# A transformer block on one core: scores in groups of three heads, V by halves, and the queue's products in column tiles

## The chip, the core and the metric

The kernel runs on one core of one Trainium2 chip. A core has a matrix engine (TensorE, PE in the profile), which reads its operands from SBUF and writes its products into PSUM; a vector engine (DVE); a scalar engine (ACT); GpSimd (POOL)[...]; and queues that start DMA transfers, here almost all from SyncE (SP). Each engine works through its own list of instructions, and semaphores order the lists among each other. [...] The metric is the time of one execution on the device in microseconds; a run's number is the median of several executions.

## The reference, cut to what matters

Attention and a feed-forward layer, each followed by a residual sum and a layer norm, over x of 4 x 2048 x 256 in fp32, 16 heads of 16 columns. The feed-forward layer rounds inputs, weights and the hidden values to FP4 in blocks of 16.

```python
q = split_heads(x @ Wq.T); k = split_heads(x @ Wk.T); v = split_heads(x @ Wv.T)
scores = jnp.einsum('bhld,bhmd->bhlm', q, k) * SCALE
attn = jax.nn.softmax(scores, axis=-1)
out = jnp.einsum('bhlm,bhmd->bhld', attn, v)
x = _layernorm(x + out.transpose(0, 2, 1, 3).reshape(B, L, D_MODEL) @ Wo.T)
gate = fp4_linear(x, w_gate); y = fp4_linear(x, w_up)
h = jax.nn.silu(gate) * y
x = _layernorm(x + fp4_linear(h, w_down))
```

## The kernel before, in words

**Steps and periods.** Attention goes by steps: one batch entry (4), one block of 512 queries (4 of them) and one group of four heads (4), 64 steps in all. Each step has 16 tiles of 128 keys (NKT), so there are 1024 periods, and each period treats one such tile, n, of one step.

**Scores twice.** The softmax is stabilised by the row maximum, and the scores are computed twice. First, `maxima` forms q rows by k columns (128 queries by 512 keys) for two heads at once into `pm`, a PSUM tile of two banks from the pool ps_m, which has two such tiles. One DVE reduce takes the maximum of both heads (line 397). `max_rows` later turns the maxima of a step round, and DMAs put them as two extra rows under q. Then `exponentials` forms the scores transposed (128 keys by 512 queries), one head to a bank of the pool ps_x (three banks), already with the maximum subtracted through the extra rows, and ACT takes the exponential (line 431) into SBUF tiles `e`, of which there are ten. The maxima run ahead of the exponentials by LEAD = 20 periods.

**Forms of the array.** The score products contract over 62 or 64 rows. Two heads stand in the upper and lower half of the array and run as a pair, which the profile shows as 62*128 and 64*128. `values` multiplies the exponentials by V: 128 keys contract, a head has 32 columns, and four heads stand next to each other in the array (128*32). They write four parts of one bank, `av`. The queue's products, such as pg, pu, pz, pq, pv and py, use the whole array (128*128), and so do nearly all transposes. An fp32 product is done in two passes, each with its own weight load, so the profile counts it twice; the score products (fp32r) take one.

**The queue.** All other work (projections, output projection and residual, feed-forward) stands in generators. `period(parts)` runs the steps that have come due, one part of each urgent generator (`max_rows`, `normalize`), and then parts of the queue until `parts` with a cost of at least LEAST have been run. `later(periods, step, rest)` puts a step off by so many calls of `period` and tells when its result may be used; `fp4` uses it between its halves. `psum` gives the queue its banks from the same three of ps_x that the exponentials use.

**The order of one period.** The loop at the end of the kernel writes this order, and each engine keeps it:

```python
for i in range(NP):
    if m < N: maxima(sm, im, i)
for i in range(NP):
    if 0 <= n < N: exponentials(s, kt, i)
    if i == 0 and n >= LAG: values(sv, kv)
...
period(1 if n >= 0 else 2)
```

On PE this is four products of maxima, two of exponentials, four of V (of the tile LAG = 2 periods back), two of exponentials, and then the queue's part.

The functions that the change touches, with the lines of the profile:

Of the kernel before, what the change touches and what calls it, by code (L numbers as in the profile page):

```python
# [31 lines left out]
F32 = mybir.dt.float32  # L32
# [18 lines left out]
FB = 16  # L51
LN_EPS = 1e-5
LEAD = 20
LAG = 2
LEAST = 300.0
PSUM = bass.MemoryType.PSUM
DRAM = bass.MemoryType.DRAM
# [16 lines left out]
def block_kernel(  # L74
# [55 lines left out]
            state["done"] = clock["now"]  # L130


    def matmul(*args, **kw):
        tc.keep_in_program_order(nc.tensor.matmul(*args, **kw))  # L134

    def transpose(*args):
        tc.keep_in_program_order(nc.tensor.transpose(*args))  # L137
# [7 lines left out]
    def fp4(pool, t, tag, gain=1.0, engine=None):  # L145

        p, nb, _ = t.shape
        amax = pool.tile([p, nb], F32, tag="amax" + tag, name="amax")
        nc.vector.tensor_reduce(amax, t, AX.X, ALU.max, apply_absolute_value=True)  # L149
        sc = pool.tile([p, nb], F32, tag="sc" + tag, name="sc")  # L150
        nc.vector.tensor_scalar(sc, amax, gain / 6.0, 1e-12, ALU.mult, ALU.max)
        rs = pool.tile([p, nb], F32, tag="rs" + tag, name="rs")
        nc.vector.reciprocal(rs, sc)
        engine = engine or nc.gpsimd
        engine.tensor_scalar(rs, rs, gain * TIES_DOWN, 1.0, ALU.mult, ALU.mult)
        xn = pool.tile([p, nb, FB], F32, tag="xn" + tag, name="xn", bufs=3 if tag else 2)
        engine.tensor_tensor(xn, t, rs.unsqueeze(2).to_broadcast([p, nb, FB]), ALU.mult)

        def rounded():
            m = pool.tile([p, nb, FB], F32, tag="m" + tag, name="m", bufs=1)  # L160
            nc.vector.tensor_single_scalar(m.bitcast(I32), xn.bitcast(I32), EXPONENT, ALU.bitwise_and)
            nc.vector.tensor_scalar(m, m, 1.0, ROUND, ALU.max, ALU.mult)  # L162
            engine.tensor_tensor(xn, xn, m, ALU.add)  # L163
            engine.tensor_tensor(xn, xn, m, ALU.subtract)  # L164
            engine.tensor_tensor(xn, xn, sc.unsqueeze(2).to_broadcast([p, nb, FB]), ALU.mult)  # L165

        return xn, later(1, rounded, 4 if tag == "" else 2)


    ident = const.tile([P, P], F32, tag="ident", name="ident")  # L170
# [178 lines left out]
            yield 900  # L349

    steps = [(b, qb, g) for b in range(B) for qb in range(NQB) for g in range(NG)]
    k_sb, q_sb, v_sb, mx_sb, av_ps, e_sb = {}, {}, {}, {}, {}, {}

    def load_q(s):
        b, qb, g = steps[s]
# [23 lines left out]
        v_sb[s] = p1.tile([P, NKT, NP * 3 * DH], F32, tag="v", name="v", bufs=2)  # L379
        nc.sync.dma_start(v_sb[s], vx[b % 2][g])  # L380

    def maxima(s, n, i):

        if n == 0 and i == 0:
            mx_sb[s] = p2.tile([P, QT, HG, NQB], F32, tag="mx", name="mx")
        kb, t = n // QT, n % QT
        pm = ps_m.tile([P, 2, QB], F32, tag="pm", name="pm")
        for j in range(2):
            rows = slice(R * j, R * j + RM)
            matmul(  # L390
                pm[:, j, :],
                q_sb[s, i][rows, t * P : (t + 1) * P],
                k_sb[s, i, kb][rows, :],
                start=True,
                stop=True,
            )
        nc.vector.tensor_reduce(mx_sb[s][:, t, 2 * i : 2 * i + 2, kb], pm, AX.X, ALU.max)  # L397

    def max_rows(s):

        nm = p2.tile([P, QT, HG], F32, tag="nm", name="nm")
        nc.vector.tensor_reduce(nm, mx_sb.pop(s), AX.X, ALU.max, negate=True)
        nh = p2.tile([P, QT, HG, 2], F32R, tag="nh", name="nh")
        nc.vector.tensor_copy(nh[:, :, :, 0], nm)
        nc.vector.tensor_tensor(nh[:, :, :, 1], nm, nh[:, :, :, 0].bitcast(F32), ALU.subtract)
        yield 0
        yield 0
        pn = psum("pn")
        for t in range(QT):
            transpose(  # L410
                pn[: 2 * HG, t * P : (t + 1) * P], nh[:, t].rearrange("p h c -> p (h c)").bitcast(F32), ident
            )
        nr = p2.tile([2 * HG, QB], F32R, tag="nr", name="nr", bufs=1)
        nc.scalar.copy(nr, pn[: 2 * HG, :])
        for i in range(NP):
            for j in range(2):
                h = 2 * i + j
                nc.sync.dma_start(
                    q_sb[s, i][R * j + RM : R * j + R, :].bitcast(F32), nr[2 * h : 2 * h + 2, :].bitcast(F32)
                )  # L420
        yield 400

    def exponentials(s, kt, i):
        kb, col = kt // QT, kt % QT * P
        pe = [psum("pe") for _ in range(2)]
        for j in range(2):
            rows = slice(R * j, R * j + R)
            matmul(pe[j], k_sb[s, i, kb][rows, col : col + P], q_sb[s, i][rows, :], start=True, stop=True)
        for j in range(2):
            e = p1.tile([P, QB], F32, tag="e", name="e", bufs=10)  # L430
            nc.scalar.activation(e, pe[j], AF.Exp, scale=SCALE)  # L431
            e_sb[s, kt, 2 * i + j] = e

    def values(s, kt):
        if kt == 0:
            av_ps[s] = ps_av.tile([P, QB], F32, tag="av", name="av")
        for j in range(HG):
            matmul(
                av_ps[s][S * j : S * j + S, :],
                v_sb[s][:, kt, (j // 2) * 3 * DH + v_at(j) : (j // 2) * 3 * DH + v_at(j) + S],  # L440
                e_sb.pop((s, kt, j)),
                start=(kt == 0),
                stop=(kt == NKT - 1),
            )

    oTs, oq_of = {}, {}
# [1 line left out]
    def normalize(s):  # L448

        av_sb = p2.tile([P, QB], F32, tag="av_sb", name="av_sb", bufs=1)  # L450
        nc.scalar.copy(av_sb, av_ps.pop(s))
        yield 0
        yield 0
        pa = psum("pa")
        for t in range(QT):
            transpose(pa[:, t * P : (t + 1) * P], av_sb[:, t * P : (t + 1) * P], ident)

        pairs = pa.rearrange("p (t i a d) -> p t i a d", t=QT, i=NP, d=DH)
        rd = p2.tile([P, QT, NP, 2], F32, tag="rd", name="rd")
        nc.vector.reciprocal(rd, pairs[:, :, :, 1:3, 0])  # L460
        if s % 2 == 0:
            oq_of[s // 2] = p2.tile([P, QT, P], F32, tag="oq", name="oq", bufs=1)
        oq = oq_of[s // 2].rearrange("p t (g i j d) -> p t g i j d", g=2, i=NP, d=DH)
        for i in range(NP):
            nc.vector.tensor_tensor(
                oq[:, :, s % 2, i],
                pairs[:, :, i, 0:4:3, :],
                rd[:, :, i, :].unsqueeze(3).to_broadcast([P, QT, 2, DH]),
                ALU.mult,
            )  # L470
        yield 500
        if s % 2 == 0:
            return
        yield 0
        pr = psum("pr")
        for t in range(QT):
            transpose(pr[:, t * P : (t + 1) * P], oq_of[s // 2][:, t, :], ident)
        oT = p1.tile([P, QB], F32, tag="oT", name="oT", bufs=3)
        nc.scalar.copy(oT, pr)
        oTs[s // 2] = oT  # L480
        yield 500
# [19 lines left out]
    def residual(b, qb, x1, xq):  # L501

        for t in range(QT):
# [10 lines left out]
            if t % 2:  # L514
                layer_norm(x1, t - 1, 2)
                tiles = x1[:, t - 1 : t + 1].rearrange("p t (b f) -> p (t b) f", f=FB)
                later(3, lambda tiles=tiles: xq.append(fp4(p2, tiles, "")))
            yield 900

    def gated(xqT, h, t, engine):  # L520
# [54 lines left out]
    def down(x1, hT, t):  # L575
        for n in range(KC):
            cols = slice(n * P, (n + 1) * P)
            pz = psum("pz")[:, :P]
            for c in range(NFC):
                w = min(P, FF - c * P)  # L580
                matmul(pz, hT[:w, t % 2, c, :], wdT[:w, c, cols], start=(c == 0), stop=(c == NFC - 1))
            nc.gpsimd.tensor_add(x1[:, t, cols], x1[:, t, cols], read(pz))  # L582
            yield 1300

    def feed_forward(b, qb, between):
# [23 lines left out]
        def gate(t):  # L609
# [2 lines left out]
            h = p2.tile([P, FF], F32, tag="h", name="h")  # L612
            yield from gated(xqT, h, t, engine)
            blocks = h.rearrange("p (b f) -> p b f", f=FB)
            later(1, lambda: hq.update({t: fp4(p2, blocks, "h", gain=0.5, engine=engine)}))

        def out_rows(t):
            layer_norm(x1, t, 2)
# [78 lines left out]
    others = [projection(0, tb, ("q0", "q1")) for tb in range(1, NQB)] + [projection(1, 0)]  # L697
    queue.append(weave(prepare(), chain_of(others), 2))

    for n in range(-LEAD, N + LAG):  # L700
        m = n + LEAD
        (sm, im), (s, kt), (sv, kv) = divmod(m, NKT), divmod(n, NKT), divmod(n - LAG, NKT)
        if m in (8, 10, 12, 14):
            if m == 8:
                load_q(1)
            load_k(1, m // 2 - 4)
        if n == 0:
            load_v(0)
        if kt == 3 and 0 <= n and s + 1 < len(steps):
            load_v(s + 1)  # L710
        if n > 0 and kt % QT == 0:
            ahead, kb = divmod(n - QT + 2 * NKT, NKT)
# [6 lines left out]
                assert (b, kb // QT, "k" + c) in projected  # L719
                load_k(ahead, kb // QT)  # L720

        for i in range(NP):
            if m < N:
                maxima(sm, im, i)
        for i in range(NP):
            if 0 <= n < N:
                exponentials(s, kt, i)
            if i == 0 and n >= LAG:
                values(sv, kv)
        if m < N and im == NKT - 1:  # L730
            urgent.append(max_rows(sm))
        if n >= LAG and kv == NKT - 1:
            urgent.append(normalize(sv))
            if sv % NG == NG - 1:
                queue.append(chain(*steps[sv][:2]))
        period(1 if n >= 0 else 2)
    banks["more"] = True
    while urgent or queue or due:
        period(1)

# [32 lines left out]
```

## Time and profile before

| What | Value |
|---|---|
| Median of the runs | 3697.28 us (3 runs, 3695.79 to 3697.76) |
| The profiled execution | 3695.37 us, span of the instructions 3693.6 us |
| Mean granted clock of PE | 0.982 |
| Busy PE, DVE, ACT, POOL | 3540.7, 2805.0, 2694.0, 1293.4 us |
| Exponentials (line 431) | 4096, 595 ns each |
| Reduces of the maxima (line 397) | 2048, 1217 ns each |

The page lists busy time by engine, then groups of instructions: line, engine, operation, tile written and tiles read, shapes, count, then busy time and the mean of one, and after the second bar the engine's idle time just before them with what ended it. PEld are the weight loads of PE, which overlap its products. The timeline lists instructions in order of time: start, duration, engine, line, operation, tiles, count, and in brackets the idle time before the first. The list of waits gives total, times and the longest.

### The profile page before, as it was taken

The numbers are of one execution on the slowest core, as the hardware profiler recorded it, in microseconds if no ns is written. First come the engines' busy times: TensorE is split into PE (matmuls) and PEld (weight loads), VectorE is DVE, ScalarE is ACT, GpSimd is POOL, SyncE is SP. The second block draws the span as 40 slices with busy tenths as digits, with TensorE's granted clock in tenths as the row PEclk, the third lists the DMA queues.
The fourth block names the chain that finished last, engine by engine and source line by source line (L and its number), as shares of the span: only waits on it lengthen the run. The fifth ranks groups of instructions, "written<-read, shape, count | busy, mean of one in ns | idle before, by whom it ended". The sixth has DMA issues, their size and how long they took to land.

```text
span 3693.6 us, 57860 instructions
## 1 busy us (share of the span) xinstructions
PE 3540.7 (96%) x21396; PEld 1602.0 (43%) x21396; DVE 2805.0 (76%) x3250; ACT 2694.0 (73%) x5452; POOL 1293.4 (35%) x1542
## 2 busy tenths in 40 slices
PE   5889999999999999999999999999999999999995
PEld 4433444444444444444444444444443434444343
DVE  3777777787787877878787787778778788878834
ACT  2667777777777777777777777777777777777772
POOL 0331432424243242423424243342424325241425
PEclk8899999999999999999999999999999999999997
DMA  6643333223232332323323232322322221222100
GB/s 217 188 137 117 93 91 105 81 85 115 68 114 84 94 94 85 109 70 109 95 78 106 85 97 88 97 89 74 113 75 63 75 79 57 75 68 86 47 7 6
DMA packets 197954, 334.18 MB, mean 90 GB/s; under 512 B 26024, under 2 KB 75560, under 8 KB 197672
## 3 DMA queue, kind: packets, MB, share of 16 engines
q1 hardware_dynamic: 196280, 329.16, 29.2%
q8 instruction: 171, 2.80, 0.3%
q10 hardware_dynamic: 1392, 1.31, 0.1%
q14 instruction: 111, 0.91, 0.1%
HBM read 242.81 MB, written 86.51 MB: 89 GB/s over the span
## 4 chain that ended last, share of the span: by engine, by line
PE 82%; DVE 11%; DMA 2%; POOL 2%; SPq 1%; issue 1%; ACT 1%; ACTq 0%; POOLq 0%; DVEq 0%
PE av L134 24%; PE pe L134 18%; PE pm L134 16%; DVE mx L397 8%; PE pz L134 5%; PE pg L134 5%; PE pu L134 5%; PE pq L134 3%; PE pth L137 1%; PE pv L134 1%; PE pa L137 1%; PE py L134 1%; PE pn L137 1%; DMA k<-kx 1%; DMA xb<-in_L_attn_x_dram 1%; DVE amax L149 1%
## 5 line engine op out<-in xcount | busy, mean ns | idle before, releaser
L397 DVE TENSOR_REDUCE mx<-pm 128x2 f32<-128x1024 f32 x2048 | 2407.9, 1217 | 706.8 <-PE pm L134 702.5
L431 ACT ACTIVATE e<-pe 128x512 f32<-128x512 f32 x4096 | 2217.9, 595 | 671.2 <-PE pe L134 666.0
L134 PE MATMUL av<-e,v 128*32 128x512 f32 x8192 | 1098.3, 608 | 0.0
L134 PE MATMUL pe<-q,k 64*128 64x512 f32 x4096 | 1037.2, 456 | 4.8 <-ACT e L431 4.4
L134 PEld LDWEIGHTS pe<-q,k 64*128 64x128 f32 x4096 | 476.4, 185 | 969.0 <-ACT e L431 855.7
L134 PE MATMUL pm<-k,q 62*128 62x512 f32 x4096 | 803.8, 448 | 60.0 <-DVE mx L397 53.0
L134 PEld LDWEIGHTS pm<-k,q 62*128 62x128 f32 x4096 | 347.0, 186 | 373.2 <-issue 178.6
L134 PEld LDWEIGHTS av<-e,v 128*32 128x32 f32 x8192 | 162.2, 108 | 332.2 <-issue 314.1
L537 POOL TENSOR_TENSOR a<-a,g 128x352 f32<-128x352 f32 x124 | 116.4, 939 | 499.5 <-ACT a L536 499.5
L582 POOL TENSOR_TENSOR x<-x,read 128x128 f32<-128x128 f32 x128 | 58.9, 460 | 493.6 <-ACT read L142 493.6
L134 PE MATMUL pz<-wdT,hT 128*128 128x128 f32 (+1 forms) x1536 | 230.0, 292 | 0.0
L163 POOL TENSOR_TENSOR xn<-xn,m 128x704 f32<-128x704 f32 (+2 forms) x104 | 159.5, 1534 | 157.7 <-DVE m L162 139.0
L134 PEld LDWEIGHTS pz<-wdT,hT 128*128 128x128 f32 (+1 forms) x1536 | 191.0, 191 | 45.5 <-ACT e L431 18.2
L551 POOL TENSOR_TENSOR h<-a,u 128x352 f32<-128x352 f32 x124 | 116.2, 937 | 226.7 <-ACT u L550 224.4
L134 PE MATMUL pg<-wgT,xqT 128*128 128x352 f32 x512 | 187.4, 489 | 0.0
L513 POOL TENSOR_TENSOR x<-x,read 128x256 f32<-128x256 f32 x64 | 46.7, 730 | 400.2 <-ACT read L142 399.9
L134 PE MATMUL pu<-wuT,xqT 128*128 128x352 f32 x512 | 186.1, 486 | 0.0
L164 POOL TENSOR_TENSOR xn<-xn,m 128x704 f32<-128x704 f32 (+2 forms) x104 | 159.8, 1536 | 5.6
L165 POOL TENSOR_TENSOR xn<-xn,sc 128x704 f32<-128x704 f32 (+2 forms) x104 | 131.5, 1264 | 7.8
L538 POOL TENSOR_TENSOR a<-a,g 128x352 f32<-128x352 f32 x124 | 118.8, 958 | 9.7
L134 PEld LDWEIGHTS pg<-wgT,xqT 128*128 128x128 f32 x512 | 88.3, 191 | 58.5 <-ACT e L431 19.1
L134 PEld LDWEIGHTS pu<-wuT,xqT 128*128 128x128 f32 x512 | 88.2, 191 | 58.7 <-ACT e L431 20.0
(95 smaller groups left out, 2283.1 us busy)
## 6 DMA issues: line engine op xcount, KB each, us to landing
k<-kx SPq DMA_DIRECT2D x1024, 128.0 KB
v<-vx SPq DMA_DIRECT2D x64, 768.0 KB
q<-qx SPq DMA_DIRECT2D x256, 124.0 KB
kx<-khi SPq DMA_DIRECT2D x64, 256.0 KB
qx<-qhi SPq DMA_DIRECT2D x64, 256.0 KB
xb<-in_L_attn_x_dram SPq DMA_DIRECT2D x27, 512.0 KB
vx<-vt SPq DMA_DIRECT2D x128, 96.0 KB
x<-in_L_attn_x_dram SPq DMA_DIRECT2D x16, 512.0 KB
```

What stands on the lines that cost most here:

```text
L134: tc.keep_in_program_order(nc.tensor.matmul(*args, **kw))
L137: tc.keep_in_program_order(nc.tensor.transpose(*args))
L163: engine.tensor_tensor(xn, xn, m, ALU.add)
L164: engine.tensor_tensor(xn, xn, m, ALU.subtract)
L165: engine.tensor_tensor(xn, xn, sc.unsqueeze(2).to_broadcast([p, nb, FB]), ALU.mult)
L397: nc.vector.tensor_reduce(mx_sb[s][:, t, 2 * i : 2 * i + 2, kb], pm, AX.X, ALU.max)
L431: nc.scalar.activation(e, pe[j], AF.Exp, scale=SCALE)
L513: nc.gpsimd.tensor_add(x1[:, t, :], x1[:, t, :], read(py[:, :D]))
L537: engine.tensor_mul(a, a, g)
L538: engine.tensor_add(a, a, g)
L551: engine.tensor_mul(h[:, cols], a, u)
L582: nc.gpsimd.tensor_add(x1[:, t, cols], x1[:, t, cols], read(pz))
```

## The change

**Groups.** The loop over periods is replaced by a loop over groups. A group issues three score products for exponentials and three for maxima, paired over the two halves of the array; `maximum` and `exponent` treat one head each. The reduce still takes two heads at once, so its tile is finished in every second or third product, now and then across two groups. Then come the three exponentials on ACT, the loads that belong to key tiles begun, a part of the queue in three groups out of four (QUEUE), and one or two halves of V (VALUES), each half being 256 of the 512 queries for four heads.

**Column tiles.** `matmul` splits a product that contracts over 128 rows and has 128 columns into four of 32 columns. Transposes stay whole.

**Smaller edits.** `later` waits 2 for 1, 5 for 4, 3 for 2 and 4 for 3 calls; `max_rows` and `normalize` wait three groups where they waited two periods; `normalize` reads `av` as soon as its last half is issued; pz takes its 64-row piece first.

```diff
-LAG = 2
+QUEUE = (1, 1, 0, 1)
+VALUES = (1, 2, 2, 1)
+EBUFS = 10
...
-    def matmul(*args, **kw):
-        tc.keep_in_program_order(nc.tensor.matmul(*args, **kw))
+    def matmul(out, lhsT, rhs, **kw):
+
+        k, m = lhsT.shape
+        parts = P // S if k == m == P else 1
+        for j in range(parts):
+            at = slice(j * m // parts, (j + 1) * m // parts)
+            tc.keep_in_program_order(nc.tensor.matmul(out[at] if parts > 1 else out, lhsT[:, at], rhs, **kw))
...
-        return xn, later(1, rounded, 4 if tag == "" else 2)
+        return xn, later(2, rounded, 5 if tag == "" else 3)
...
+    def maximum(p):
+
+        m, h = divmod(p, HG)
+        (s, n), (i, j) = divmod(m, NKT), divmod(h, 2)
...
+        if j == 0:
+            pm_of[p // 2] = ps_m.tile([P, 2, QB], F32, tag="pm", name="pm")
...
+        if j == 1:
+            nc.vector.tensor_reduce(mx_sb[s][:, t, 2 * i : 2 * i + 2, kb], pm_of.pop(p // 2), AX.X, ALU.max)
...
-        yield 0
-        yield 0
+        for _ in range(3):
+            yield 0
...
+    def exponent(p):
+
+        n, h = divmod(p, HG)
+        (s, kt), (i, j) = divmod(n, NKT), divmod(h, 2)
         kb, col = kt // QT, kt % QT * P
+        pe = psum("pe")
+        rows = slice(R * j, R * j + R)
+        matmul(pe, k_sb[s, i, kb][rows, col : col + P], q_sb[s, i][rows, :], start=True, stop=True)
+
+        def exponentials():
+            e = p1.tile([P, QB], F32, tag="e", name="e", bufs=EBUFS)
+            nc.scalar.activation(e, pe, AF.Exp, scale=SCALE)
+            e_sb[s, kt, h] = e
+
+        return exponentials
+
+    def values(s, kt, half):
...
+        cols = slice(half * QB // 2, (half + 1) * QB // 2)
         for j in range(HG):
             matmul(
+                av_ps[s][S * j : S * j + S, cols],
                 v_sb[s][:, kt, (j // 2) * 3 * DH + v_at(j) : (j // 2) * 3 * DH + v_at(j) + S],
+                (e_sb.pop((s, kt, j)) if half else e_sb[s, kt, j])[:, cols],
+
+                start=(kt == 0 and half == 0),
+                stop=(kt == NKT - 1 and half == 1),
             )
...
-                later(3, lambda tiles=tiles: xq.append(fp4(p2, tiles, "")))
+                later(4, lambda tiles=tiles: xq.append(fp4(p2, tiles, "")))
...
-            for c in range(NFC):
+
+            for c in (NFC - 1, *range(NFC - 1)):
                 w = min(P, FF - c * P)
-                matmul(pz, hT[:w, t % 2, c, :], wdT[:w, c, cols], start=(c == 0), stop=(c == NFC - 1))
+                matmul(pz, hT[:w, t % 2, c, :], wdT[:w, c, cols], start=(c == NFC - 1), stop=(c == NFC - 2))
...
-            later(1, lambda: hq.update({t: fp4(p2, blocks, "h", gain=0.5, engine=engine)}))
+            later(2, lambda: hq.update({t: fp4(p2, blocks, "h", gain=0.5, engine=engine)}))
...
+    pes = deque(range(N * HG))
+    halves = deque((n, half) for n in range(N) for half in range(2))
+    g, given = 0, 0
+    while halves:
+        ready = given
+        rows, begun = [[], []], []
+        for _ in range(min(3 if g else 2, len(pes))):
+            p = pes.popleft()
+            begun += [p // HG] if p % HG == 0 else []
+            rows[p % 2].append((exponent, p))
+            given += 1
+        for _ in range(min(3, len(pms))):
+            p = pms.popleft()
+            rows[p % 2].append((maximum, p))
+        work = []
+        for i in range(max(len(r) for r in rows)):
+            for product, p in (r[i] for r in rows if i < len(r)):
+                if product is exponent:
+                    work.append((p, exponent(p)))
+                else:
+                    maximum(p)
+                    maxima_done(p)
+        for p, step in sorted(work, key=lambda x: x[0]):
+            step()
+
+        for n in begun:
+            loads(n)
+        period(QUEUE[g % 4])
+        for _ in range(VALUES[g % 4] if pes else 4):
+            if halves and halves[0][0] * HG + HG <= ready:
+                n, half = halves.popleft()
+                values(*divmod(n, NKT), half)
...
```

More of the change, by code (lines that the diff above doesn't have):

```diff
@@ L351, in block_kernel @@
     steps = [(b, qb, g) for b in range(B) for qb in range(NQB) for g in range(NG)]
-    k_sb, q_sb, v_sb, mx_sb, av_ps, e_sb = {}, {}, {}, {}, {}, {}
+    k_sb, q_sb, v_sb, mx_sb, av_ps, e_sb, pm_of = {}, {}, {}, {}, {}, {}, {}
     def load_q(s):
@@ L380, in load_v @@
         nc.sync.dma_start(v_sb[s], vx[b % 2][g])
-    def maxima(s, n, i):
-        if n == 0 and i == 0:
+    def maximum(p):
+        m, h = divmod(p, HG)
+        (s, n), (i, j) = divmod(m, NKT), divmod(h, 2)
+        if n == 0 and h == 0:
             mx_sb[s] = p2.tile([P, QT, HG, NQB], F32, tag="mx", name="mx")
+        if j == 0:
+            pm_of[p // 2] = ps_m.tile([P, 2, QB], F32, tag="pm", name="pm")
         kb, t = n // QT, n % QT
[L387 to L397, printed above, removed]
+        rows = slice(R * j, R * j + RM)
+        matmul(
+            pm_of[p // 2][:, j, :],
+            q_sb[s, i][rows, t * P : (t + 1) * P],
+            k_sb[s, i, kb][rows, :],
+            start=True,
+            stop=True,
+        )
+        if j == 1:
+            nc.vector.tensor_reduce(mx_sb[s][:, t, 2 * i : 2 * i + 2, kb], pm_of.pop(p // 2), AX.X, ALU.max)
     def max_rows(s):
@@ L421, in max_rows @@
         yield 400
-    def exponentials(s, kt, i):
+    def exponent(p):
+        n, h = divmod(p, HG)
+        (s, kt), (i, j) = divmod(n, NKT), divmod(h, 2)
         kb, col = kt // QT, kt % QT * P
[L425 to L435, printed above, removed]
+        pe = psum("pe")
[7 more added lines that the diff above has]
+    def values(s, kt, half):
+        if kt == 0 and half == 0:
             av_ps[s] = ps_av.tile([P, QB], F32, tag="av", name="av")
+        cols = slice(half * QB // 2, (half + 1) * QB // 2)
         for j in range(HG):
             matmul(
-                av_ps[s][S * j : S * j + S, :],
+                av_ps[s][S * j : S * j + S, cols],
                 v_sb[s][:, kt, (j // 2) * 3 * DH + v_at(j) : (j // 2) * 3 * DH + v_at(j) + S],
-                e_sb.pop((s, kt, j)),
-                start=(kt == 0),
-                stop=(kt == NKT - 1),
+                (e_sb.pop((s, kt, j)) if half else e_sb[s, kt, j])[:, cols],
+                start=(kt == 0 and half == 0),
+                stop=(kt == NKT - 1 and half == 1),
             )
@@ L451, in normalize @@
         nc.scalar.copy(av_sb, av_ps.pop(s))
-        yield 0
-        yield 0
+        for _ in range(3):
+            yield 0
         pa = psum("pa")
@@ L698, in block_kernel, with loads @@
     queue.append(weave(prepare(), chain_of(others), 2))
[L700 to L706, printed above, removed]
+    def loads(n):
+        s, kt = divmod(n, NKT)
         if n == 0:
             load_v(0)
-        if kt == 3 and 0 <= n and s + 1 < len(steps):
+        if kt == 3 and s + 1 < len(steps):
             load_v(s + 1)
@@ L720, in block_kernel @@
                 load_k(ahead, kb // QT)
[L722 to L735, printed above, removed]
@@ L736, in block_kernel, with maxima_done @@
-        period(1 if n >= 0 else 2)
+    def maxima_done(p):
+        if (p + 1) % (NKT * HG) == 0:
+            urgent.append(max_rows(p // (NKT * HG)))
+    pms = deque(range(N * HG))
+    for m in range(LEAD):
+        if m in (8, 10, 12, 14):
+            if m == 8:
+                load_q(1)
+            load_k(1, m // 2 - 4)
+        for _ in range(HG):
+            maximum(pms[0])
+            maxima_done(pms.popleft())
+        period(2)
+    pes = deque(range(N * HG))
+    halves = deque((n, half) for n in range(N) for half in range(2))
@@ new lines, in block_kernel @@
+    g, given = 0, 0
[27 more added lines that the diff above has]
+                values(*divmod(n, NKT), half)
+                if half and n % NKT == NKT - 1:
+                    sv = n // NKT
+                    heads = normalize(sv)
+                    next(heads)
+                    urgent.append(heads)
+                    if sv % NG == NG - 1:
+                        queue.append(chain(*steps[sv][:2]))
+        g += 1
```

## The prediction

> **What bounds the kernel now.** I read the page's busy table first, then the costliest groups, then the timeline of a steady stretch around 2000 us, the list of waits, and last the busy time by stretches.
>
> ```profile
> span 3693.6 us, 57860 instructions
> ...
> PE 3540.7 (96%) x21396; PEld 1602.0 (43%) x21396; DVE 2805.0 (76%) x3250; ACT 2694.0 (73%) x5452; POOL 1293.4 (35%) x1542
> ...
> L397 DVE TENSOR_REDUCE mx<-pm 128x2 f32<-128x1024 f32 x2048 | 2407.9, 1217 | 706.8 <-PE pm L134 702.5
> L431 ACT ACTIVATE e<-pe 128x512 f32<-128x512 f32 x4096 | 2217.9, 595 | 671.2 <-PE pe L134 666.0
> ...
> L134 PE MATMUL pm<-k,q 62*128 62x512 f32 x4096 | 803.8, 448 | 60.0 <-DVE mx L397 53.0
> ```
>
> PE is the bound: ACT and DVE idle mostly for PE, and PE lost only 53 us to the maxima. But 96% is not 96% of useful streaming. The timeline of PE shows one whole period:
>
> ```profile
> 2000.95 0.50 PE L134 MATMUL pe<-q,k 64*128 64x512 f32 x2
> 2001.39 1.45 PE L134 MATMUL pu<-wuT,xqT 128*128 128x352 f32 x4
> 2002.77 0.73 PE L134 MATMUL pm<-k,q 62*128 62x512 f32 x4
> 2003.34 0.40 PE L134 MATMUL pe<-q,k 64*128 64x512 f32 x2
> 2003.67 1.06 PE L134 MATMUL av<-e,v 128*32 128x512 f32 x8
> 2004.66 0.49 PE L134 MATMUL pe<-q,k 64*128 64x512 f32 x2
> 2005.09 0.66 PE L137 MATMUL pa<-ident,av_sb 128*128 128x128 f32 x4
> ```
>
> Start to start gives the prices. Three pairs of score products (2002.77 to 2003.67) take 0.90 us; a lone pair (2004.66 to 2005.09) 0.43. So a pair streams 0.23 us, and one visit to this form of the array costs 0.20 beside it. V (2003.67 to 2004.66) takes 0.99. A queue part of four passes of 352 columns takes 1.38, 4 x 0.293 of it streaming and again 0.20 around it. These visits are what the change goes for.
>
> The same stretch on DVE, and what ended the waits of DVE's smaller operations in the whole run:
>
> ```profile
> 2003.31 2.36 DVE L397 TENSOR_REDUCE mx<-pm 128x2 f32<-128x1024 f32 x2 [1.35 <-PE pm L134]
> 2005.79 0.26 DVE L460 RECIPROCAL rd<-pa 128x16 f32<-128x16 f32 x1
> 2006.08 0.49 DVE L465 TENSOR_TENSOR oq<-pa,rd 128x128 f32<-128x128 f32 x2
> ```
>
> ```profile
> DVE rd L460 <- PE pa L137: 52.0, 33, 24.5
> ...
> DVE st L489 <- POOL x L582: 30.0, 6, 8.0
> ...
> DVE amax L149 <- POOL h L551: 17.1, 2, 15.3
> ```
>
> Two reduces take 2.36 us of a period of some 3.3 to 3.7, about one idle us is left, and the other DVE work and its waits for POOL fall into that hole. That is why PE barely notices DVE now. Last, two neighbouring stretches, with the granted clock as the sixth value after the stretch's length:
>
> ```profile
> 3212.40:3215.80 3.40, 1.86 (x12) 0.67 (x8) 3.40 (x6) 1.52 (x3) 2.79 (x6) 1.00 0.00 0
> 3215.80:3219.20 3.40, 3.40 (x18) 1.38 (x16) 2.68 (x7) 1.78 (x4) 1.61 (x3) 0.52 0.27 77
> ```
>
> Where PE is held 1.5 us in 3.4, with DVE full, the next stretch runs at half clock.
>
> **What the Trainium skill says.** "TensorEngine Tiling (Array Packing)", Key Properties: changing the tiling mode drains TensorE, and different tiles run in parallel. The trace agrees: 0.20 us per visit, and four V products of 32 columns share one stream. "TensorE: Matmul & The Clock Gate", LDWEIGHTS: a load costs its columns divided by 1.2 per ns, 107 ns for 128 and 27 for 32. That agrees: 1.38 less 4 x 0.293 leaves 0.107 load and some 0.095 drain, and V's 0.99 is 0.854 streaming, 0.027 load and 0.115 drain. The same page, Part 1: an idle window drops the clock to half, as above (0.52). The same page, on queue depths: VectorE and ScalarE are strict FIFO, so an operation that waits there holds everything behind it.
>
> **The change part by part.** *Fewer visits, column tiles.* The order of the built program gives 3998 changes of array form before and 3155 after: a group is one row-tiled block (three pairs), then queue and V in column tiles together. With a drain of 0.095 (0.115 after column tiles) and a load of 0.107 (0.027 for 32 columns) they cost 720 us before and 551 after: **-170 us**. The streaming stays: queue 847 us (512 passes each of pg and pu at 0.296, 512 of pq at 0.216, 256 each of pv and py at 0.216, 1536 of pz at 0.111, some 1390 transposes at 0.109), V 2048 halves of 0.427, scores 4096 pairs of 0.23. That a 128-column product split into four tiles streams as one is shown only by V; bounds: -60 us (pz is then bound by streaming, not by its load), +150 us if issue holds the 128-column ones back. V's eight loads and eight products start within 50 ns, so I take 0. pz's short chunk put first keeps the row form: inside the count.
>
> *The queue's bank.* ps_x has three banks and a group takes all three for its exponentials. The queue part after them gets the bank of the group's first one. That is free at 0.107 + 0.23 + 0.20 (pair to ACT: 2000.95 to 2001.49 less load and stream) + 0.595 + 0.05 = 1.18 us after the block's start, and PE is ready at 0.90. Before, the bank three back was that of an earlier exponential, long done. 0.28 us x 906 queue visits (1024 less 118 periods without) = **+254 us**; 0 to 290.
>
> *The maxima by threes.* 1.5 reduces a group. A PM tile of two banks is begun in an even group and finished in the odd one after it, and so holds one of only two buffers meanwhile. In an odd group both reduces end about 0.77 + 2 x 1.12 + 0.1 = 3.1 us after the block's start, and the third pair of the next block needs the second of them, at 0.57: odd to even takes at least 2.6 us. Naturally an odd group with queue, one half of V and the bank's wait takes 2.3 + 0.28, with two halves 3.0. So the loop is just closed, with no hole left. All DVE work between now counts where it is longer than its cover: by the four places of the cycle 1.0, 1.27, 0.46 and 1.55 us. The pieces by the groups' rows, 384 of them: quantizing h 64 x 1.49 and 64 x 1.19, x1 32 x 1.2 and 32 x 0.86, LayerNorm 64 x 1.18, row maxima 64 x 0.87, normalize 64 x 0.83. With 0.34 each of their own waiting (130 us in the list: 52 + 37 + 17 and smaller), the excess over the covers, meaned over the four places, is 160 us; 53 is paid already: **+110**, 0 to 250.
>
> *Their waits grow.* bn_stats waits for POOL's add behind an ACT read that now stands behind three exponentials; amax(h) waits for POOL, which does 12.2 us of work for four gate parts in 4 x 3.3 us. If waits grow by half, **+65**; 0 to 200. The longer lags (2 for 1, 5 for 4, 4 for 3, in shorter groups) hold about the same real time. What is queued behind them is the reduces, and for these waits PE.
>
> *The clock.* Holds of 1.5 us come more often; some 15 half-clock stretches at 1.7 us: **+25**; 0 to 100.
>
> *At nothing.* loads(n) issues the same DMAs as late as before on SP, after the group's work; K comes 28 periods (some 90 us) ahead, so even a whole group's delay is covered. POOL's queue issues none. max_rows and normalize, three groups for two periods, wait 2.25 periods. EBUFS is the old 10.
>
> Sum: -170 + 254 + 110 + 65 + 25 = +284. The profiled span is 3693.6; its execution took 3695.4, and the median of the runs is 1.9 above that. 3693.6 + 284 + 3.7 = 3981: **3980 us**.
>
> **The rivals.** *All waits hidden:* PE is as bound as now and only the visits count: 3527 us. For it: ACT and DVE idle 670 and 700 us for PE. Against it: two reduces already fill two thirds of a period, and the bank's arithmetic. It decides where PE's new waits stay under 170/1366 = 0.12 us a group, and it is the rival on the other side. Half of the bank's wait gives 3650. *The bank's wait alone, DVE in time:* 3697 + 84 = 3780: the 0.28 is paid, the small DVE work lands in groups held up anyway. *Clock:* holds gather in windows, some 100 half-clock stretches: 4150. *That queue products do not share the array:* 847 us would be paid up to four times; V speaks against it.
>
> **How the numbers follow.** Forecast (3880 to 4110) 0.60; bank alone (3705 to 3880) 0.17; hidden 0.13; clock or worse 0.08; no difference 0.02. A difference under 0.2% can't be told from none. Faster 0.13, same 0.02, slower 0.85. Range 3740 to 4110: it leaves out the hidden case, the edge of the bank case and the clock case.
>
> **What would show it.** Idle before pm products ended by DVE mx rising from 53 to over 250 us; idle of queue products ended by ACT e; DVE st and amax waiting for POOL some 100 us or more; PE's share below 92%. Against me: DVE idle for PE as large as now and PE at 96%. I would be wrong if reduces end earlier than 1.12 us apart, or if queue parts seldom meet a bank still in use.

## The result, and the profile after

The changed kernel takes 4052.75 us (median of 4 runs, 4049.72 to 4055.85), the kernel before 3697.48 in the same comparison: a ratio of 1.0962, 95% interval 1.0943 to 1.0981. That is 355 us more. The forecast was 3980 with 3740 to 4110.

The page of the changed kernel, with the rows that answer to those shown of before:

```profile
span 4047.9 us, 94421 instructions
...
PE 3577.4 (88%) x39572; PEld 1732.8 (43%) x39572; DVE 2847.3 (70%) x3250; ACT 2664.5 (66%) x5452; POOL 1295.4 (32%) x1542
...
L407 DVE TENSOR_REDUCE mx<-pm 128x2 f32<-128x1024 f32 x2048 | 2436.2, 1219 | 767.1 <-PE pm L141 709.8
L444 ACT ACTIVATE e<-pe 128x512 f32<-128x512 f32 x4096 | 2159.6, 598 | 752.4 <-PE pe L141 740.3
L141 PE MATMUL pm<-k,q 62*128 62x512 f32 x4096 | 1053.9, 432 | 222.7 <-DVE mx L407 204.4
```

The busy times of the engines are within 2% of those before (PE 3577 us for 3541, DVE 2847 for 2805), over a span that is 354 us longer: all of them idle more. The reduces on DVE and the exponentials on ACT wait 710 and 740 us for PE (703 and 666 before), and PE waits 204 us for DVE where it waited 53: they wait for each other by turns. A share of 96% or 88% tells little about what holds the engines; the list of waits tells more:

```profile
PEld pm L141 <- DVE mx L407: 395.4, 530, 10.1
...
PE pm L141 <- DVE mx L407: 204.4, 269, 9.8
...
DVE st L507 <- POOL x L601: 87.5, 62, 9.2
...
DVE amax L156 <- POOL h L569: 76.7, 62, 14.7
...
DVE st L507 <- POOL x L531: 69.7, 58, 3.4
...
PEld pz L141 <- ACT e L444: 68.1, 108, 0.9
PEld pg L141 <- ACT e L444: 64.9, 119, 0.7
...
DVE amax L156 <- POOL x L515: 45.9, 22, 3.2
```

The first two are weight loads (PEld) and products (PE) that wait for late reduces; the two overlap and can't be added. Then come small DVE operations that wait for POOL, three lines and the last one. The remaining two are queue products that wait for ACT to give back a bank. In the kernel before, the smaller parts of the small operations' waits were these, beside the 30.0 of st and the 17.1 of amax that the prediction shows:

```profile
DVE st L489 <- POOL x L513: 7.2, 18, 3.4
...
DVE amax L149 <- POOL x L497: 4.1, 2, 2.2
```

So the waits of st for POOL went from 37 to 157 us and those of amax from 21 to 123. One place shows a small operation and a late reduce at once. The timeline of the changed kernel:

```profile
1109.32 0.73 PE L141 MATMUL pe<-q,k 64*128 64x512 f32 x3
1109.66 0.40 PE L141 MATMUL pm<-k,q 62*128 62x512 f32 x1
1109.75 1.10 POOL L515 TENSOR_SCALAR x<-x,minus,rstd 128x256 f32<-128x256 f32 x2
...
1110.89 0.69 DVE L156 TENSOR_REDUCE amax<-x 128x32 f32<-128x512 f32 x1 [2.51 <-POOL x L515]
1111.49 1.22 DVE L407 TENSOR_REDUCE mx<-pm 128x2 f32<-128x1024 f32 x1
...
1112.76 0.79 PE L141 MATMUL pm<-k,q 62*128 62x512 f32 x2 [2.71 <-DVE mx L407]
```

At 1109.66 PE writes another of the maxima's products, done by 1110.06. DVE's next instruction is not the reduce but amax of x1, which waits for the layer norm on POOL until 1110.89; the reduce starts behind it at 1111.49. PE needs the buffer that this reduce frees and stands for 2.71 us. What follows is in the stretches of the same trace, where the granted clock is again the sixth value after the length:

```profile
1108.60:1112.00 3.40, 1.45 (x20) 0.52 (x12) 1.11 (x2) 2.12 (x5) 2.06 (x5) 1.00 0.19 49
1112.00:1118.80 6.80, 6.04 (x44) 2.67 (x48) 5.10 (x9) 1.95 (x4) 2.00 (x3) 0.50 0.10 30
```

PE was busy 1.45 of 3.4 us, and then has half its clock for 6.8 us. From 330 us after the start to 140 us before the end, the clock records of the trace add up to 136.5 us at half clock, where the kernel before had 10.2.

### The profile page after: what moved, and what is told of

Same layout as the page of the kernel before. It is cut to its first block, busy times and chain, and to the rows that moved or that the text cites. A ratio compares the mean times of both kernels' runs of the same rounds, so it can differ in the third digit from the quotient of the medians.

```text
span 4047.9 us, 94421 instructions
## 1 busy us (share of the span) xinstructions
PE 3577.4 (88%) x39572; PEld 1732.8 (43%) x39572; DVE 2847.3 (70%) x3250; ACT 2664.5 (66%) x5452; POOL 1295.4 (32%) x1542
## 4 chain that ended last, share of the span: by engine, by line
PE 53%; DVE 19%; ACT 9%; POOL 9%; issue 3%; DMA 2%; POOLq 0%; ACTq 0%; SPq 0%; DVEq 0%
PE av L141 16%; DVE mx L407 14%; PE pe L141 12%; ACT e L444 7%; PE pm L141 6%; PE pz L141 5%; PE pg L141 4%; PE pu L141 4%; POOL xn L164 2%; PE pq L141 1%; DVE amax L156 1%; DVE m L168 1%; POOL h L569 1%; POOL x L515 1%; PE pth L144 1%
## 5 line engine op out<-in xcount | busy, mean ns | idle before, releaser
L444 ACT ACTIVATE e<-pe 128x512 f32<-128x512 f32 x4096 | 2159.6, 598 | 752.4 <-PE pe L141 740.3
L141 PE MATMUL pm<-k,q 62*128 62x512 f32 x4096 | 1053.9, 432 | 222.7 <-DVE mx L407 204.4
L141 PE MATMUL av<-e,v 128*32 128x256 f32 x16384 | 1176.6, 390 | 0.0
L141 PE MATMUL pe<-q,k 64*128 64x512 f32 x4096 | 1112.7, 479 | 38.4 <-ACT e L444 30.5
L141 PEld LDWEIGHTS pm<-k,q 62*128 62x128 f32 x4096 | 502.8, 188 | 433.7 <-DVE mx L407 395.4
L141 PEld LDWEIGHTS av<-e,v 128*32 128x32 f32 x16384 | 454.8, 111 | 448.7 <-issue 289.2
L141 PE MATMUL pz<-wdT,hT 128*32 128x128 f32 (+1 forms) x5376 | 222.0, 281 | 23.4 <-ACT e L444 20.9
L141 PEld LDWEIGHTS pz<-wdT,hT 128*32 128x32 f32 (+1 forms) x5376 | 173.1, 115 | 88.5 <-ACT e L444 68.1
L141 PE MATMUL pg<-wgT,xqT 128*32 128x352 f32 x2048 | 180.0, 470 | 18.4 <-ACT e L444 16.5
L141 PE MATMUL pu<-wuT,xqT 128*32 128x352 f32 x2048 | 177.8, 465 | 8.6 <-ACT e L444 6.9
L149 ACT COPY read<-pz 128x128 f32<-128x128 f32 x128 | 34.1, 266 | 132.1 <-PE pz L141 132.1
```

The lines of the kernel that those rows point to most:

```text
L141: tc.keep_in_program_order(nc.tensor.matmul(out[at] if parts > 1 else out, lhsT[:, at], rhs, **kw))
L444: nc.scalar.activation(e, pe, AF.Exp, scale=SCALE)
```

## The experiments

All ratios are to the kernel before on the same chip, with 95% intervals. Differences in us are between medians; on the chips used, the kernel before had medians of 3697.5 to 3698.7.

**1. Column tiles alone.** The old order of a period with the new `matmul`.

```diff
-    def matmul(*args, **kw):
-        tc.keep_in_program_order(nc.tensor.matmul(*args, **kw))
+    def matmul(out, lhsT, rhs, **kw):
+        k, m = lhsT.shape
+        parts = P // S if k == m == P else 1
+        for j in range(parts): ...
```

> The old order of a period, with the queue's products split into four column tiles and nothing else. If four tiles stream as one (my forecast): the same number of visits, each of some 900 queue visits loads 32 columns for 128 and saves up to 0.08 us, 60 to 70 us less at most, part of it lost again to DVE, so 3630 to 3690 us. If tiles do not share the array, or if issue holds them: pg, pu, pq and the like take far longer than their 847 us of streaming, 3800 us or more. Four products of one pass should start within some 25 ns of each other.

Measured: 3687.35 us, 0.9969 (0.9958 to 0.9981), the fastest version with the whole computation, 0.3% ahead of the kernel before. Its timeline of PE:

```profile
2005.86 1.39 PE L139 MATMUL pg<-wgT,xqT 128*32 128x352 f32 x16
2007.18 0.73 PE L139 MATMUL pm<-k,q 62*128 62x512 f32 x4
```

A queue visit of four 352-column passes, now 16 products, takes 1.32 us start to start where pu took 1.38. So four column tiles stream as one, and the shorter load shows. 900 visits by 0.06 would give 54 us; 11 arrive. PE's busy time falls by 31 us (3540.7 to 3509.3) and its span by 9; its weight loads for the maxima now wait 239 us for DVE, 169 before. So much of what PE saves it waits again, and its time at half clock grew too, from 10.2 to 34.1 us.

**2. The changed kernel with whole products.** The reverse edit, in the changed kernel.

> The changed kernel with whole queue products, as before. If column tiles do what they are for: about 570 more changes of form (3722 for 3155), each 0.15 to 0.2 us, 60 to 110 us more, 4110 to 4160. If the column tiles themselves are what made the changed kernel slow: less than 4053, towards 3800.

Measured: 4111.45, 1.1116 (1.1099 to 1.1133). Column tiles are worth 59 us in the new groups. They are not what made the kernel slow.

**3. V ahead of the queue.**

```diff
-        period(QUEUE[g % 4])
         for _ in range(VALUES[g % 4] if pes else 4):
...
+        period(QUEUE[g % 4])
...
-            for c in (NFC - 1, *range(NFC - 1)):
+            for c in range(NFC):
```

> The changed kernel with V's halves ahead of the queue's part in each group (and pz's 64-row piece last, so that it still stands next to the scores). Theory A, as the prediction has it: the queue waits 0.28 us for the bank of the group's first exponential; V is 0.43 to 0.85 us of cover for that, so up to 254 us less, 3800 to 3900. Theory B: three banks are too few whatever the order; the queue's bank is then read later and the next group's exponentials wait for it instead: no gain or a loss, 4050 to 4200, with PE waiting for ACT before pe products 300 us or more.

Measured: 4205.85, 1.1372 (1.1355 to 1.1389), 153 us more: theory B, and even a little beyond its range. Its groups on the page:

```profile
L141 PE MATMUL pe<-q,k 64*128 64x512 f32 x4096 | 1309.4, 492 | 152.6 <-ACT a L554 48.7
...
L141 PE MATMUL pg<-wgT,xqT 128*32 128x352 f32 x2048 | 177.3, 464 | 0.0
```

The queue's product pg no longer waits (18.4 us in the changed kernel, 0.0 here), and the exponentials' products wait 152.6 where they waited 38.4, now also for the queue's reader (a). That is half of the 300 us expected, and PE's idle time as a whole is no longer than in the changed kernel (464.3 us for 470.5). The rest of the loss stands inside PE's busy time, because the modelled end of a product covers a short hold. The timeline has one block of scores with such a hold:

```profile
2002.06 0.51 PE L141 MATMUL pe<-q,k 64*128 64x512 f32 x2
2002.89 0.49 PE L141 MATMUL pe<-q,k 64*128 64x512 f32 x1 [0.33 <-ACT read L149]
```

The third product of the group starts 0.83 us after the first, when ACT has read the queue's bank; 0.33 of that is listed as idle. Changing the order moves the wait from the queue to the exponentials and doesn't take it away.

**4. DVE in the order of the code.** The compiler's scheduling may let an instruction pass others on its engine; PE's are pinned in the code, DVE's are not. Here DVE's are pinned too.

```diff
+    class Pinned:
+        def __getattr__(self, name):
+            op = getattr(nc.vector, name)
+            return lambda *args, **kw: tc.keep_in_program_order(op(*args, **kw))
+
+    vector = Pinned()
...
-            nc.vector.tensor_reduce(...)
+            vector.tensor_reduce(...)
```

> The changed kernel with every DVE operation kept in the order in which the code writes it, where the compiler's own scheduling otherwise lets small operations pass ahead of reduces. If the growth of waits comes from small operations that wait for POOL in front of ready reduces: waits of st and amax for POOL fall from 280 us to under 100 and the time by 100 to 150, to 3900 to 3950. If those waits are a result and not a cause: 4050 give or take 20.

Measured: 3909.02, 1.0571 (1.0553 to 1.0588): 144 us less. The list of waits, where operations of DVE now bear the wrapper's line:

```profile
PEld pm L148 <- DVE mx L94: 271.4, 483, 4.5
...
PE pm L148 <- DVE mx L94: 99.6, 189, 4.2
...
DVE st L94 <- POOL x L608: 27.9, 5, 8.7
...
DVE st L94 <- POOL x L538: 16.9, 19, 3.4
```

PE's wait for reduces halves, st waits 45 us for 157, and the waits of amax are gone from the top of the list. At half clock there are 34 us for 136.5. So the order that the scheduler gave DVE, with small operations ahead of ready reduces, was a cause. The sentence ahead of the prediction that each engine keeps the loop's order holds for PE and not for DVE.

**5. Maxima in twos and fours.** A PM tile never stays half filled from one group to the next; the price is a pair's slot in every second group.

```diff
-        for _ in range(min(3, len(pms))):
+        for _ in range(min(4 if g % 2 else 2, len(pms))):
...
-        if j == 0:
+        first = p // 2 not in pm_of
+        if first:
...
-        if j == 1:
+        if not first:
```

> The changed kernel with two maxima in one group and four in the next instead of three and three, so that a PM tile never stays half filled from one group to the next. It costs one pair's slot more per two groups, 683 x 0.23 = 157 us of streaming. If the half-filled tile, which holds one of two buffers over a group, is a main cause of PE's waits for the maxima: the time falls in spite of it, by 80 to 150, to 3900 to 3970, and PE waits for DVE mx well less than now. If not: 4053 + 157 = 4210, or some 4150 with part of the slots hidden.

Measured: 3925.32, 1.0615 (1.0599 to 1.0631): 127 us less, although the added slots are 157 us of streaming by count. The page:

```profile
L141 PE MATMUL pm<-k,q 62*128 62x512 f32 x4096 | 1109.9, 416 | 119.9 <-DVE mx L408 107.7
```

PE's wait for the reduces falls from 204 to 108 us. The threes, with their tile held over a group, are a main cause. The longer groups also give ACT more time to free the queue's bank (the weight loads of pz, pg, pq and pu wait 188 us for e, 238 in the changed kernel), so not all of the gain need be the tile's.

**6. Both.**

> Both at once: even groups of maxima and DVE in the written order. If the two causes are separate: their gains nearly add, 3820 to 3860. If both remove the same waits: no better than the better of the two alone, 3905.

Measured: 3845.36, 1.0399 (1.0383 to 1.0414), 207 less than the changed kernel, of 271 if the gains simply added: three quarters of that sum. The page's group of the maxima's products, now at 39.9 us of waiting for DVE:

```profile
L148 PE MATMUL pm<-k,q 62*128 62x512 f32 x4096 | 1093.9, 412 | 50.9 <-DVE mx L94 39.9
```

DVE holds PE far less than in the changed kernel (39.9 us for 204), and 148 us over the kernel before remain.

**7. Reduces over half of the keys**, with DVE in the order of the code.

```diff
-            vector.tensor_reduce(..., pm_of.pop(p // 2), AX.X, ALU.max)
+            vector.tensor_reduce(..., pm_of.pop(p // 2)[:, :, : QB // 2], AX.X, ALU.max)
```

> The changed kernel with DVE in the written order, and each reduce of the maxima over 256 of the 512 keys only (a part of the maximum is left out), which takes some 0.55 us off each of 2048 reduces. If what remains over the version with DVE in the written order (3909) is waiting for DVE: 150 to 200 less, 3700 to 3760. If it is ACT and the queue's bank: 3850 to 3900. Only the change's saving of visits, with no waits at all, would be near 3530.

Measured: 3706.19, 1.0023 (1.0015 to 1.0031): 203 less than experiment 4. A reduce now takes 687 ns for 1218. With that work gone, the new groups just about reach the kernel before; 179 us lie between that and the 3527 of the case in which all waits are hidden.

**8. The kernel before, DVE in the order of the code.**

> The kernel before with every DVE operation in the written order. If the written order is simply better on DVE: faster, 3600 to 3680. If the scheduled order suits the old period and only the new groups upset it: 40 to 80 slower, 3735 to 3780.

Measured: 3740.12, 1.0112 (1.0096 to 1.0129). The scheduled order helps the old period by 42 us and costs the new groups 144.

**9 to 12. Banks.** Four kernels, two of each order of work, all with DVE in the order of the code. A bank here is a PSUM tile of 512 fp32 values per partition; the kernel's pools hold eight of them, two PM tiles of two, one for av and three in ps_x. In these runs only one head of each pair has its maximum formed, so that a PM tile is one bank; two banks come free, and stay unused or go to ps_x. PE keeps its slots, since the remaining product of a pair streams as long as both did; a reduce takes 685 or 686 ns for some 1217. Four kernels first planned for the same question, with the maxima over 256 of the 512 keys, gave no times.

```diff
-    ps_x = ctx.enter_context(tc.tile_pool(name="ps_x", bufs=3, space=PSUM))
+    ps_x = ctx.enter_context(tc.tile_pool(name="ps_x", bufs=5, space=PSUM))
...
-            pm_of[p // 2] = ps_m.tile([P, 2, QB], F32, tag="pm", name="pm")
+            pm_of[p // 2] = ps_m.tile([P, QB], F32, tag="pm", name="pm")
...
+        if j == 0:
             matmul(
...
-            nc.scalar.activation(e, pe, AF.Exp, scale=SCALE)
+            nc.scalar.activation(e, pe, AF.Exp, scale=SCALE / 16)
```

> The changed kernel, DVE in the written order, with the maxima of only one head of each pair (the other head's maxima are left out, and the exponent is scaled by a sixteenth so that it stays finite). A PM tile then takes one bank for two and a reduce half its elements; PE still has three slots in a group, since the lone products keep theirs. ps_x keeps three banks, two banks of PSUM stay unused. It is the base of the next run, and should be near the run with half reduces (3706): 3680 to 3730.

> The same with the two freed banks given to ps_x, five for three. If waiting for banks (the queue's 0.28 us, and the next group's exponentials behind the queue's readers on ACT) is what is left: 250 to 320 less, 3380 to 3450, and hardly a wait of PE for ACT. If PE's streaming and visits are what is left: within 50 of the run with three.

> The kernel before with the same edits (DVE in the written order, maxima of one head of each pair, exponent scaled) and three banks: 3650 to 3700, at or below the changed kernel with three, since its products reuse banks later.

> The same with five banks. If the prediction's 170 us for fewer visits are a true gain that DVE and the banks ate: 3550 to 3600, and 130 to 200 above the changed kernel with five. If the gain is not there at all: within 30 of the changed kernel with five, or below it.

| Maxima of one head, DVE in the order of the code | three banks | five banks | five for three |
|---|---|---|---|
| new groups | 3698.56, 1.0003 (0.9994 to 1.0011) | 3385.67, 0.9156 (0.9142 to 0.9170) | -312.9 |
| old periods | 3666.25, 0.9913 (0.9898 to 0.9928) | 3554.31, 0.9608 (0.9594 to 0.9623) | -111.9 |
| new less old | +32.3 | -168.6 | |

The waits of queue products for ACT in the new groups with three banks:

```profile
PEld pz L148 <- ACT e L452: 75.5, 120, 0.9
PEld pg L148 <- ACT e L452: 74.3, 119, 0.7
PEld pq L148 <- ACT e L452: 63.4, 109, 0.7
PEld pu L148 <- ACT e L452: 59.4, 120, 0.7
```

With five, of these four one is left, and pu waits a little for a reader of the queue's own:

```profile
PEld pu L148 <- ACT a L562: 21.6, 59, 0.4
...
PEld pq L148 <- ACT e L452: 4.0, 12, 0.7
```

With five banks and DVE at two thirds of its load, the new groups are 168.6 us faster than the old periods. In neither of these two runs does PE wait much: from 330 us after the start to 140 us before the end it is busy 2893.3 of 2911 us (new) and 3075.5 of 3083 us (old). The starts of products say the same. From the first product of a block of scores to the next product of another form, the median in the new groups is 1.18 us with three banks and 0.90 with five, which is the prediction's price for three pairs and one visit. The idea of the change is sound. Nothing in the kernel as it stands gives those banks: this arrangement leaves half of the maxima out.

The old order gains too, 112 us, though its list of waits names hardly any for a bank on PE (pe for e, 4.4 us in the kernel before). The trace of before shows where, just behind the period whose prices the prediction took:

```profile
2005.68 0.73 PE L134 MATMUL pm<-k,q 62*128 62x512 f32 x4
2006.25 0.57 PE L134 MATMUL pe<-q,k 64*128 64x512 f32 x2
...
2006.76 1.07 PE L134 MATMUL av<-e,v 128*32 128x512 f32 x8
```

The three pairs take 1.08 us here, behind the short queue part pa, where they took 0.90 behind pu. With one head's maxima, blocks behind pa take 1.08 us in the median with three banks and 0.90 with five, and in periods without a queue part the scores gain more. So after a short queue part, or none, the exponentials of the old order wait for a bank, again inside PE's modelled busy time. Summed over the same part of both traces, the blocks of scores account for about 100 of the 112 us.

## Why the prediction was right, and where it was not

The time lies in the range, 73 us above the forecast of 3980. Of the signs that it named, PE's share below 92% (88), the waits of st and amax for POOL (157 and 123 us) and queue products waiting for ACT's e came true; PE's wait for the reduces came to 204 us, short of the 250. The pairs of runs split the 355 us, each as the new order's change less the old one's:

| Step | From the runs | us | In the prediction |
|---|---|---|---|
| Fewer visits to a form of the array | five banks, one head's maxima: new less old | -168.6 | -170 |
| Three banks for five | 312.9 - 111.9 | +201 | +254 (0 to 290) |
| Both heads' maxima on DVE | (3909.0 - 3698.6) - (3740.1 - 3666.3) | +137 | +110 (0 to 250) |
| DVE's scheduled order, and the clock | (4052.75 - 3909.0) + (3740.1 - 3698.2) | +186 | +65 and +25 |
| Sum | | +355 | +284 |

It is one order of splitting; in another, the shares of DVE and banks would differ, since both hold PE at the same moments (experiment 6). The last two rows are set beside the terms that come nearest to them; the steps of the runs and the terms of the sum are not the same cuts.

**Fewer visits: right.** The count of changes of form by drain and load came out within 2 us, in a pair of runs in which PE hardly waits. That it is so close is partly luck: by its own figures the two drains are 0.101 and 0.109 us (1.38 - 1.172 - 0.107 and 0.99 - 0.854 - 0.027), where it writes 0.095 and 0.115, and 0.01 us on each of 843 visits is 8 us. The split into load and drain has support outside that sum: the profile's records of loads of 128 and of 32 columns last 191 and 108 ns, which are 83 apart, as the 107 and 27 are 80 apart. The streaming it uses, 0.293 us for 352 columns, follows from the trace of before, where four passes of 352 columns take 1.38 us and four of 256 take 1.06 (pq, 1501.45 to 1502.51): 0.83 ns a column. One reading is wrong and changes nothing: of V's eight products, only four at a time start together, and the second four follow 0.45 us later. Experiment 1 settles what the trace of before could show only for V: four column tiles of a whole product share one stream (1.32 us for 1.38).

**The queue's bank: right in kind, wrong in both of its sizes, and near by luck.** The new groups lose 313 us to having three banks, not 254, and more than the 290 at the edge of the term's range. What the prediction named only as the queue's wait is a shortage: put V in its place, and the exponentials wait instead. And the old order, in which it took the bank three back to be long done and put the wait at nothing, loses 112 us. The two errors go the same way, and so the difference, 201, comes within 53 us of the term.

**The maxima by threes: right.** 137 for 110, or by its own parts 210 for 160 in the new groups and 74 for 53 paid already in the old. Experiment 5 shows the half-filled tile in it, and experiment 7 the load on DVE.

**Their waits grow: right in direction, mis-sized.** Waits and clock together were put at 90 us and came to 186; that is 96 too low, against 53 too high for the bank. The prediction asked why the small operations start late and let their waits grow by half. It did not ask where they stand among the reduces: the text ahead of it has each engine keep the order of the loop. On DVE the order is the scheduler's. In the changed kernel it puts amax ahead of a reduce whose product is there already (1109.66), and the waits of st for POOL went from 37 to 157 us, those of amax from 21 to 123, four to six times for one and a half. Pinned in the order of the code, the kernel gets 144 us back. That the scheduler places them by what it expects of PE, and expects it wrong, is argued and not shown; that the order costs the time is shown.

**The clock: counted too low.** 136.5 us at half clock, against some 15 stretches of 3.4 us (51 us) in the forecast. At half clock at most half of such time is lost, so at most 68 us here, 17 with DVE pinned (34.1 us at half clock) and 5 before. It lies inside the +186 and can't be taken apart from it by these runs, since in the changed kernel, over the stretch of time named above, each of the 26 times at half clock follows 3.4 us in which PE was busy 2.0 us or less.

**The rival in which all waits are hidden** (3527) is out, and the runs say at what price it would hold: five banks and light reduces bring 3386, but against an old order that gets 3554 from the same gifts. **The rival of the bank's wait alone** (3780) is out as well: DVE is not in time, as experiments 4, 5 and 7 show.

## What to carry to other kernels

An engine at 96% may be paying for switches and drains that hide the latency of the others. Before taking these out, ask which buffers, banks and reduces were in time only because of them, since these may come next: here 169 us of switches were saved, and 524 us of other time came in. Count PSUM banks per group against the time from a product to the end of its reader, in the old order as well as in the new, and compare starts of products, since a short hold can stand inside the modelled busy time. Keep a tile from staying half filled across a group. And look at the order that the built program really has on each engine, not at that of the code: one small operation that waits ahead of a ready one holds everything behind it on that engine.

## What the runs showed of the hardware

A product of 128 columns in fp32, split into four of 32 columns, costs no more PE time than the whole one: 1.32 us for 1.38 for four passes of 352 columns, with 16 products for four.

Half clock came after stretches of 3.4 us in which PE was busy in part: 1.45 us of it in the changed kernel (1108.6, one hold of 2.71 us), 1.86 us in the kernel before (3212.4, held twice, for 0.84 and 0.70 us). Such holds cost twice, once as the wait and once as slow PE after it. The changed kernel's records of the clock change on a grid of 3.41 us. Of the stretches of that grid at full clock, from 330 us after the start to 140 us before the end, half clock followed all 18 with PE busy 1.63 us or less, and of those with 1.69 to 2.0 us some and not others: the stretch of 3593.5 to 3596.9, with 1.69 us, kept the full clock after it. So an idle window, which is how the prediction put it, need not be idle throughout.
